# Two cross-attention layers on one core: the second layer's 256 query channels with a batch in each of two banks, projections ahead of the first layer's transposes, sums ahead of their copies

## The chip, the core and the metric

The kernel runs on one core of a Trainium2 chip, alone. The core has five engines with an instruction queue each: TensorE (PE; its weight loads are listed as PEld), VectorE (DVE), ScalarE (ACT), GpSimd (POOL) and SyncE (SP), which here only issues DMAs. The metric is the device time of one execution in microseconds (us); lower is better. Times of a kernel are given as the median of several executions.

## The reference

64 batches of 256 positions with 320 channels go through two cross-attention layers, one after the other, each with 20 heads of 16 channels and a context of 77 tokens with 512 channels.

```python
# layer 0
q = heads(x @ Wq.T); k = heads(ctx @ Wk.T); v = heads(ctx @ Wv.T)
x = merge(softmax(q k^T / 4) v) @ Wo.T + bo + x
# (its four "image" tokens are an empty slice here)

# layer 1: 73 text tokens, 4 image tokens
q = heads(x @ W_q); k_t, v_t = text @ W_k, text @ W_v; k_ip, v_ip = image @ W_k_ip, image @ W_v_ip
probs_t  = softmax(q k_t^T / 4)
text_out = probs_t v_t
sem      = l2norm(probs_t @ text) @ l2norm(image)^T
probs_ip = softmax(q k_ip^T / 4 + 0.5 * sem) * spatial_mask
out = (text_out + probs_ip v_ip) @ W_out + b_out + x
```

## The kernel before, in words

**Layout.** Channels lie on partitions. Batches are taken in pairs `p` (32 pairs). Of the 320 channels, 256 are two full tiles of 128 (`main`), and the last 64 of both batches of a pair share one tile (`last`: batch 0 in rows 0 to 63, batch 1 in rows 64 to 127). Weights have four tiles of input channels: two of 128, and two for the last 64, padded with zeros to 128 rows (rows 0 to 63 filled in one, rows 64 to 127 in the other), so that either batch can be picked out of `last` with a full K=128 matmul.

**Steps.** The main loop (L1065) runs over steps `g`. A period of ten steps (`NU`) handles one pair; `k = g % 10`, `p = g // 10`. In each step layer 0 handles one unit of pair `p` (8 heads of 128 positions; units 0 to 4 of batch 0, then of batch 1), and layer 1 handles the unit that layer 0 had 13 steps (`LAG`) before. So layer 1's units of pair `p-1` begin in `k = 3` of period `p`. A step issues, in this order: what earlier steps left (`drains`: copies of first-layer queries, or the addition after a projection); the matmuls into one four-bank tile `sc` (`semantics` of layer 1's previous unit, L755 and L761, then `scores` of both layers, L641); `shifted` on DVE (maximum and difference, L659 and L661, for each layer); layer 1's `transposed` (L705, L706, copied out by ACT at L712, L713); layer 0's exponential (L669; after layer 0's transposes in `k = 5`); `weighted` (L772, L775, DVE); the `first` fillers; layer 0's `transposed` (L705, copied out at L731, L732 or L720, L723); the copy of the sums out of `sc` (L1114, ACT, which waits until DVE's L775 is done with the tile); layer 1's exponentials (L672, L673); `normalize` (L687 and L688 on DVE, L692 on POOL); the `second` fillers; `attend` after a unit that completes a group; the `third` fillers; and after the last unit of a batch `image_norm`, which loads ACT's square-root table and then the exponential table again (L874, L876).

**Fillers.** All work that is done once per pair is spread over the steps by `fillers` (L956), a table written by hand: for each `k`, which function stands in which place (0 first, 1 second, 2 third) and for which pair.

**Order.** Engines run their instructions in the order in which the program issues them (`keep_order` at the end binds PE, ACT, DVE and POOL to it). An engine that waits holds up everything behind it in its own queue.

**PSUM.** The score tile `sc` has four banks and one buffer: the next step's `semantics` may write it only once DVE and ACT have read it. Transposes use the pool `ptr` with two banks, everything else (keys, values, queries, projections, gram matrices, `pv` of `attend`) the pool `pms` with two banks, taken in turn. So the user after next of a bank waits for whatever empties it.

**Queries.** `first_queries` (L577) makes layer 0's 256 main channels by `halves` (L520): one bank per batch, sixteen PE records at L528 over the two full tiles of input channels, and then, kept back until the start of the next step, eight records at L537, where each batch's half of `last` is a K=64 matmul in its own rows of the array. `queries(l, p, m)` (L547) makes one tile `m` of output channels at a time in one bank for both batches (L555, L557, with the zero-padded K=128 weights for `last`); `m = 2` are the last 64 channels (L563, L570). Layer 1 uses `queries` for all three tiles, layer 0 for the last one. (A matmul of these fp32 operands leaves two records.)

**Others named below.** `gram` (L484) makes a product of the context with itself that layer 1's `semantics` needs: matmuls at L493, two ACT copies, three POOL operations, one DMA at L502 and eight at L506; `place_gram` (L509) puts it into `gv` and `gr` on POOL. `project` (L590) is the output projection by `halves`, with its addition on DVE (L601) at the start of the next step; `project_last` (L609) is that of the last 64 channels, added at L620. `keys` (L326), `keys_by_head` (L360, POOL), `place_values` (L415, POOL) and `attend` (L778) are what they say. `keep_busy` (L734) issues transposes of the identity whose results nobody reads; it is used only after the last pair has entered.

Of the kernel before, what the change touches and what calls it, by code (L numbers as in the profile page):

```python
# [8 lines left out]
F32 = mybir.dt.float32  # L9
# [9 lines left out]
S = 256  # L19
T = 77  # L20
NIP = 4
TT = T - NIP
P = 128
# [14 lines left out]
HT = H - 4  # L38
NU = 2 * len(UNITS)
LAG = NU + 3  # L40
SCALE = D**-0.5
SEM = 0.5
EPS = 1e-12
# [20 lines left out]
def tile_two_cross_attentions(ctx: ExitStack, tc: tile.TileContext, a: dict, out: bass.AP):  # L64
# [35 lines left out]
    nc = tc.nc  # L100
# [443 lines left out]

    held = {}

    def queries(l, p, m):  # L547

        main, last = xts[p]
        ps = pms.tile([P, 512], F32, tag="ms", name=f"q_ps{l}_{p}_{m}")  # L550
        if m < 2:
            q = qs[l, p, m] = big.tile([P, S2], F32, tag=f"q{l}{m}", name=f"q{l}_{p}_{m}", bufs=1)
            c = slice(m * P, (m + 1) * P)
            for i in range(2):
                nc.tensor.matmul(ps, wq[l][:, i, c], main[:, i, :], start=(i == 0), stop=False)  # L555
            for b in range(2):
                nc.tensor.matmul(ps[:, b * S : (b + 1) * S], wq[l][:, 2 + b, c], last, start=False, stop=(b == 1))  # L557
            nc.scalar.copy(q, ps)
            return
        to = [ps[s * HALF : (s + 1) * HALF, :S].rearrange("p (b t) -> p b t", b=2) for s in range(2)]  # L560
        for i in range(2):
            for s in range(2):
                nc.tensor.matmul(  # L563
                    to[s], wq[l][:, i, C - HALF :],
                    main[:, i, :].rearrange("p (b s t) -> p b s t", b=2, s=2)[:, :, s, :],
                    start=(i == 0), stop=False,
                )
        for b in range(2):
            for s in range(2):
                nc.tensor.matmul(  # L570
                    to[s][:, b, :], wq[l][:, 2 + b, C - HALF :], last[:, s * P : (s + 1) * P],
                    start=False, stop=(b == 1),
                )
        q = qs[l, p, 2] = big.tile([P, 2, P], F32, tag=f"q{l}2", name=f"q{l}_{p}_2", bufs=1)
        nc.scalar.copy(q.rearrange("p b t -> p (b t)"), ps[:, :S])

    def first_queries(p):  # L577

        rest = halves(f"q_ps0_{p}", wq[0], xts[p])

        def end():
            ps = rest()
            q = big.tile([P, 2, S2], F32, tag="q0", name=f"q0_{p}")
            for m in range(2):
                qs[0, p, m] = q[:, m, :]
            return [lambda b=b: nc.scalar.copy(q[:, :, b * S : (b + 1) * S], ps[b]) for b in range(2)]  # L586

        held["q"] = end

    def project(l, p):  # L590

# [37 lines left out]
    def eight(t, u):  # L629

        return t[:, PLACES[u] : PLACES[u] + 8].rearrange("p (r e) ... -> p r e ...", e=2)
# [102 lines left out]
    def keep_busy(n):  # L734


        if n:
            ps = ptr.tile([P, 4, P], F32, tag="tr", name=f"busy{len(busy)}")
            busy.append(n)
            for i in range(n):  # L740
                nc.tensor.transpose(ps[:, i % 4, :], ident, ident)
# [24 lines left out]
    def by_block(ps):  # L766
        return ps[:, :, SEM0 : SEM0 + 2 * GV].rearrange("p r (e t) -> p r e t", t=GV)
# [93 lines left out]
    def image_least(p, b):  # L861


        total = stats[p, b][1][:, :, NIP + D]
        t = least[p, b] = small.tile([P, 2 * H], F32, tag="least", name=f"least{p}_{b}", bufs=1)
        nc.gpsimd.tensor_mul(t, total, total)
# [89 lines left out]
    def fillers(k, p):  # L956


        f = ([], [], [], [])

        def add(half, q, fn, *args):
            if 0 <= q < NP:
                f[half].append((fn, args))

        if k == 0:
            if p == 0:
                for l in range(2):
                    add(0, p, value_rows, 0, l)
                add(1, p, values, 0, p, 0)
            add(0, p - 1, gram, p - 1, 0)  # L970
            add(0, p - 3, project_last, 1, p - 3)
            add(2, p - 2, text_transposed, p - 2, 0)
            if p:
                add(2, p, place_values, 0, p, 0)
            add(2, p - 1, values, 1, p - 1, 0)
        elif k == 1:
            if p == 0:
                for l in range(2):
                    add(l, p, value_rows, 1, l)
                add(1, p, place_values, 0, p, 0)  # L980
            add(0, p, queries, 0, p, 2)
            add(1, p - 1, project, 0, p - 1)
            add(1, p - 1, place_gram, 0)
            add(1, p, keys_by_head, 0, p, 1)
            add(1, p - 1, keys_by_head, 1, p - 1, 0)
        elif k == 2:
            if p == 0:
                for i in range(2):
                    add(0, p, keys, 1, p, i)
            add(0, p - 1, project_last, 0, p - 1)  # L990
            add(1, p + 1, load_x, p + 1)
            add(1, p - 1, queries, 1, p - 1, 0)
            add(1, p - 1, place_values, 1, p - 1, 0)
            add(1, p, values, 0, p, 1)
        elif k == 3:
            add(0, p + 1, load_context, p + 1)
            add(0, p - 1, queries, 1, p - 1, 2)
            if p == 0:
                add(1, p, image_keys, 0)
            add(1, p - 1, queries, 1, p - 1, 1)  # L1000
            add(1, p, place_values, 0, p, 1)
            add(1, p - 1, keys_by_head, 1, p - 1, 1)
        elif k == 4:
            if p == 0:
                add(0, p, image_keys, 1)
            else:
                add(0, p, keys, 1, p, 0)
            add(1, p - 1, values, 1, p - 1, 1)
            add(1, p + 1, first_queries, p + 1)
        elif k == 5:  # L1010
            if p == 0:
                add(0, p, image_keys, 2)
            add(0, p + 1, keys, 0, p + 1, 0)
            add(2, p - 2, text_transposed, p - 2, 1)
        elif k == 6:
            while len(made_rows) * P < min(NB, 2 * (p + 2)) * T:
                rows_todo.extend((len(made_rows), l) for l in range(2))
                made_rows.append(rows_todo[-1])
            for n in range(len(rows_todo) // 2):
                add(0, p, value_rows, *rows_todo.pop(0))  # L1020
            if p == 0:
                add(0, p, image_norms)
            else:
                add(1, p, keys, 1, p, 1)
            add(1, p - 1, gram, p - 1, 1)
            add(1, p, place_image_keys, p)
        elif k == 7:
            add(0, p + 1, keys, 0, p + 1, 1)
            add(1, p + 1, last_keys, p + 1)
            add(1, p - 2, lambda: made.update(wT=image_transposed(p - 2)))  # L1030
            add(1, p - 1, place_values, 1, p - 1, 1)
            add(1, p - 1, image_values, p - 1, 0)
            if p == 0:
                add(1, p, image_rows)
        elif k == 8:
            while rows_todo:
                add(0, p, value_rows, *rows_todo.pop(0))
            add(1, p - 1, place_gram, 1)
            add(1, p + 1, keys_by_head, 0, p + 1, 0)
            add(1, p - 1, image_values, p - 1, 1)  # L1040
            add(1, p - 2, image_attend_last, p - 2)
            add(3, p - 2, lambda: held.update(i=lambda: image_attend(p - 2)))
        else:
            add(0, p - 2, project, 1, p - 2)
            add(1, p + 1, values, 0, p + 1, 0)
            for b in range(2):
                add(1, p - 1, place_image_values, p - 1, b)
        return f
# [7 lines left out]
        keys(0, 0, i)  # L1056
    last_keys(0)
    keys_by_head(0, 0, 0)
    first_queries(0)
    for fn in held.pop("q")():  # L1060
        fn()

    last0 = last1 = before1 = None
    later, early = {}, {}
    for g in range(NP * NU + LAG + 12):  # L1065
# [23 lines left out]
            drains += held.pop("i")()  # L1089
        for fn in drains:  # L1090
            fn()
        for l in range(2):
            if now[l]:
                shifted(ps, l, *now[l])
# [7 lines left out]
            prod = weighted(ps, *before1[:4])  # L1102
        for fn, args in first:
            fn(*args)
        if last0:
            transposed(0, *last0)
        idle = g - NP * NU
        if idle > 2:
            keep_busy(14 if now[1] else {13: 12, 14: 16, 15: 14, 16: 16, 17: 16}.get(idle, 0))
        if now[0] and k == 5:  # L1110
            exponential(0, g, *now[0])
        ends = before1 and before1[2] == len(UNITS) - 1
        if before1:
            nc.scalar.copy(eight(stats[before1[:2]][1], before1[2]), by_block(ps)[:, :, :, TT:])  # L1114
            if ends:
                image_least(*before1[:2])
        if now[1]:
            exponential(1, g, *now[1])
        for fn, args in later.pop(g, ()):
# [76 lines left out]
```

## Time and profile before

| | us |
|---|---|
| median of 3 runs | 2626.64 (2626.13 to 2627.05) |
| the profiled execution's own time | 2627.7 |
| its span in the profile | 2626.0 |
| mean granted TensorE clock | 0.996 of full speed |
| a period of ten steps in the middle (1206.56 to 1284.43) | 77.87 |

The costliest groups of the profile that the change bears on (line, engine, what, busy us in all, mean ns of one):

| line | what | records | busy us | mean ns |
|---|---|---|---|---|
| L555 | second-layer queries, full tiles, both batches (PE) | 256 | 120.6 | 593 |
| L557 | second-layer queries, padded last 64 (PE) | 256 | 68.8 | 391 |
| L528 | first-layer queries by `halves` (PE) | 512 | 116.9 | 380 |
| L537 | first-layer queries, last 64, K=64 (PE) | 256 | 36.3 | 402 |
| L493 | gram (PE) | 512 | 45.2 | 231 |
| L1114 | copy of the sums (ACT) | 320 | 96.6 | 302 |
| L874, L876 | table loads (ACT) | 128 | 164.2 | 1283 |
| L620 | addition of the last 64 channels (DVE) | 64 | 30.5 | 476 |

How to read it: the busy time of PE records overlaps, since matmuls are pipelined and their ends are modelled; the time that a group takes on PE is better read as the distance from its first start to the start of what follows. A step's length is the distance between the first L755 of two steps.

### The profile page before, as it was taken

The numbers are of one execution on the slowest core, as the hardware profiler recorded it, in microseconds if no ns is written. First come the engines' busy times: TensorE is split into PE (matmuls) and PEld (weight loads), VectorE is DVE, ScalarE is ACT, GpSimd is POOL, SyncE is SP. The second block draws the span as 40 slices with busy tenths as digits, with TensorE's granted clock in tenths as the row PEclk, the third lists the DMA queues.
The fourth block names the chain that finished last, engine by engine and source line by source line (L and its number), as shares of the span: only waits on it lengthen the run. The fifth ranks groups of instructions, "written<-read, shape, count | busy, mean of one in ns | idle before, by whom it ended". The sixth has DMA issues, their size and how long they took to land.

```text
span 2626.0 us, 74027 instructions
## 1 busy us (share of the span) xinstructions
PE 2558.2 (97%) x27006; PEld 1981.0 (75%) x27006; DVE 1972.3 (75%) x3641; ACT 1539.2 (59%) x3989; POOL 1440.1 (55%) x3514
## 2 busy tenths in 40 slices
PE   7999999999999999999999999999999999999998
PEld 5677777777777777777777777777777777777676
DVE  3577777777777777777777777777777777777764
ACT  3465665665665665665665665665665665665553
POOL 2455555565555566555566555566555556555542
PEclk9999999999999999999999999999999999999999
DMA  5212211112111112211112111112211112211000
GB/s 163 72 29 58 58 42 47 42 51 57 51 50 47 43 51 56 58 43 47 42 52 57 51 50 47 42 52 57 56 46 47 42 52 56 55 41 36 26 22 23
DMA packets 154657, 132.26 MB, mean 50 GB/s; under 512 B 48248, under 2 KB 132984, under 8 KB 154296
## 3 DMA queue, kind: packets, MB, share of 16 engines
q1 hardware_dynamic: 153432, 126.38, 17.9%
q8 instruction: 216, 3.54, 0.6%
q14 instruction: 145, 1.19, 0.2%
q10 hardware_dynamic: 864, 1.15, 0.1%
HBM read 89.53 MB, written 33.91 MB: 47 GB/s over the span
## 4 chain that ended last, share of the span: by engine, by line
PE 85%; DVE 7%; ACT 3%; DMA 2%; issue 1%; POOL 1%; SPq 1%; DVEq 0%; POOLq 0%; ACTq 0%
PE sc L755 12%; PE tr L705 11%; PE o_ps L528 8%; PE sc L641 7%; PE v_ps L379 6%; PE sc L761 4%; PE q_ps L528 4%; PE q_ps L555 4%; PE k_ps L334 4%; PE o_ps L616 3%; PE o_ps L537 3%; PE pv L788 2%; DVE w L661 2%; PE q_ps L563 2%; PE q_ps L557 2%; DVE mx L659 2%
## 5 line engine op out<-in xcount | busy, mean ns | idle before, releaser
L659 DVE TENSOR_REDUCE mx<-sc 128x8 f32<-128x584 f32 (+1 forms) x640 | 497.8, 778 | 461.1 <-PE sc L641 461.1
L692 POOL TENSOR_TENSOR parts<-w,sm 128x512 f32<-128x512 f32 (+1 forms) x640 | 439.7, 708 | 299.8 <-ACT parts L673 180.7
L661 DVE TENSOR_TENSOR w<-sc,mx 128x616 f32<-128x616 f32 x640 | 512.0, 800 | 66.7 <-DVE mx L659 0.5
L712 ACT COPY pt<-tr 128x512 f32<-128x512 f32 x320 | 186.8, 584 | 446.6 <-PE tr L705 435.0
L705 PE MATMUL tr<-ident,parts 128*128 128x128 f32 x2560 | 410.4, 283 | 11.1 <-POOL parts L692 5.3
L755 PEld LDWEIGHTS sc<-gv,pt 64*128 64x128 f32 x5120 | 317.9, 188 | 108.8 <-ACT sums L1114 60.3
L755 PE MATMUL sc<-gv,pt 64*128 64x94 f32 x5120 | 357.6, 279 | 27.9 <-ACT sums L1114 27.7
L705 PEld LDWEIGHTS tr<-ident,parts 128*128 128x128 f32 x2560 | 283.0, 141 | 122.2 <-issue 87.0
L676 POOL COPY att<-w 128x32 f32<-128x32 f32 x320 | 66.8, 209 | 471.9 <-DVE w L661 471.4
L669 ACT ACTIVATE w<-w 128x616 f32<-128x616 f32 x320 | 232.0, 725 | 96.8 <-DVE w L661 96.2
L687 DVE TENSOR_REDUCE sm<-w 128x8 f32<-128x616 f32 x320 | 248.6, 777 | 14.0 <-ACT w L669 14.0
L641 PE MATMUL sc<-kbd,q 32*128 32x154 f32 x5120 | 248.5, 306 | 1.0 <-ACT q L586 0.8
L528 PE MATMUL o_ps<-aT,wo 128*128 128x256 f32 x1024 | 233.4, 381 | 0.0
L1125 DVE TENSOR_REDUCE nrm<-prod 128x8 f32<-128x584 f32 x320 | 227.6, 711 | 0.4
L772 DVE TENSOR_TENSOR prod<-sc,parts 128x512 f32<-128x512 f32 x320 | 218.0, 681 | 4.0 <-PE sc L761 4.0
L528 PEld LDWEIGHTS o_ps<-aT,wo 128*128 128x128 f32 x1024 | 190.7, 191 | 24.0 <-DVE aT L934 0.4
L672 ACT ACTIVATE parts<-w 128x512 f32<-128x512 f32 x320 | 206.8, 646 | 0.0
L641 PEld LDWEIGHTS sc<-kbd,q 32*128 32x128 f32 x5120 | 187.3, 187 | 6.0 <-issue 5.0
L731 ACT COPY pt<-tr 128x512 f32<-128x512 f32 x256 | 150.6, 588 | 67.4 <-PE tr L705 66.7
L379 PE MATMUL v_ps<-wv,cf 128*128 128x320 f32 (+1 forms) x624 | 182.1, 438 | 0.0
L706 PE MATMUL rtr<-ident,parts 128*104 128x128 f32 (+1 forms) x640 | 175.0, 273 | 0.0
L1114 ACT COPY sums<-sc 128x168 f32<-128x168 f32 x320 | 96.6, 302 | 120.2 <-DVE prod L775 119.0
(151 smaller groups left out, 4838.5 us busy)
## 6 DMA issues: line engine op xcount, KB each, us to landing
vip<-vip_rows SPq DMA_DIRECT2D x1280, 5.0 KB
out_dram<-x SPq DMA_DIRECT2D x64, 256.0 KB
x<-in_x_dram SPq DMA_DIRECT2D x31, 512.0 KB
v_rows<-vs SPq DMA_DIRECT2D x38, 320.0 KB
vm<-v_rows SPq DMA_DIRECT2D x152, 80.0 KB
ct<-in_ctx_dram SPq DMA_DIRECT2D x32, 308.0 KB
cf<-in_ctx_dram SPq DMA_DIRECT2D x38, 256.0 KB
g_rest<-gram_rest SPq DMA_DIRECT2D x512, 0.5 KB
```

The source lines that it names most:

```text
L379: nc.tensor.matmul(ps[:n, :C], cfs[i][:, k, :n], wv[l][:, k, :], start=(k == 0), stop=(k == KE - 1))
L528: nc.tensor.matmul(ps[b][:, m, :], w[:, k, m * P : (m + 1) * P], main[:, k, b * S : (b + 1) * S], start=(k == 0 and m == 0), stop=False,)
L641: nc.tensor.matmul(ps[:, r, 2 * T * l : 2 * T * (l + 1)], q[rows, b, :] if part == 2 else q[rows, t0 : t0 + P], kbd[rows, part].rearrange( ...
L659: nc.vector.tensor_reduce(mx, sc[:, :, :, :nt], AX.X, ALU.max)
L661: nc.vector.tensor_tensor(w, sc, mx.unsqueeze(3).broadcast_to([P, 4, 2, T]), ALU.subtract)
L669: nc.scalar.activation(w, w, AF.Exp, scale=SCALE)
L687: nc.vector.tensor_reduce(sm, w, AX.X, ALU.add)
L692: nc.gpsimd.tensor_tensor(two[:, 8 * t0 : 8 * t1].rearrange("p (h t) -> p h t", h=8), w[:, :, t0:t1], sm.unsqueeze(2).broadcast_to([P, 8, ...
L705: nc.tensor.transpose(ps[:, i, :], flat[:, i * P : (i + 1) * P], ident)
L755: nc.tensor.matmul(ps[:, i % 2 * 2 + j, at : at + GV], pt[half_rows, i, :], gv[b][half_rows, part, i, :], start=start and i < 2, stop=False,)
L772: nc.vector.tensor_tensor(prod[:, :, :, :M], sm[:, :, :, :M], w[:, :4].rearrange("p (e a) j t -> p (a j) e t", e=2), ALU.mult)
L1125: nc.vector.tensor_reduce(eight(stats[q, b][2], u), prod, AX.X, ALU.add)
```

## The change

Five edits. Second-layer queries of the main 256 channels use `halves`, with one bank per batch, in one piece at the end of `k = 2` instead of a tile each in `k = 2` and `k = 3`; the function is now `queries(l, p)`, and that of the last 64 channels `last_queries(l, p)`. In `fillers`, work is moved: `gram` of batch 0 from `k = 0` to `k = 2`, `place_gram(0)` from `k = 1` to `k = 3`, the first layer's last queries from `k = 1` to `k = 3`, `project(0)` in `k = 1` and the first-layer queries in `k = 4` from behind the first layer's transposes to ahead of them, the second batch's `keys_by_head` from `k = 3` to `k = 2`, and the second layer's first tile of keys from `k = 4` to `k = 3`. In the steps `LONG` (1, 4, 8 and 9) the copy of the sums is issued ahead of the first layer's transposes and their copies. In the tail one filler (the transposes of the last pair's image weights) is issued earlier, with eight more idle transposes behind it.

```diff
+LONG = (1, 4, 8, 9)
...
-    def queries(l, p, m):
+    def last_queries(l, p):
         main, last = xts[p]
-        ps = pms.tile([P, 512], F32, tag="ms", name=f"q_ps{l}_{p}_{m}")
-        if m < 2:
-            q = qs[l, p, m] = big.tile([P, S2], F32, tag=f"q{l}{m}", name=f"q{l}_{p}_{m}", bufs=1)
-            c = slice(m * P, (m + 1) * P)
-            for i in range(2):
-                nc.tensor.matmul(ps, wq[l][:, i, c], main[:, i, :], start=(i == 0), stop=False)
-            for b in range(2):
-                nc.tensor.matmul(ps[:, b * S : (b + 1) * S], wq[l][:, 2 + b, c], last, start=False, stop=(b == 1))
-            nc.scalar.copy(q, ps)
-            return
+        ps = pms.tile([P, 512], F32, tag="ms", name=f"q_ps{l}_{p}_2")
...
-    def first_queries(p):
-        rest = halves(f"q_ps0_{p}", wq[0], xts[p])
+    def queries(l, p):
+        rest = halves(f"q_ps{l}_{p}", wq[l], xts[p])
         def end():
             ps = rest()
-            q = big.tile([P, 2, S2], F32, tag="q0", name=f"q0_{p}")
+            q = big.tile([P, 2, S2], F32, tag=f"q{l}", name=f"q{l}_{p}", bufs=2 - l)
             for m in range(2):
-                qs[0, p, m] = q[:, m, :]
+                qs[l, p, m] = q[:, m, :]
             return [lambda b=b: nc.scalar.copy(q[:, :, b * S : (b + 1) * S], ps[b]) for b in range(2)]
-        held["q"] = end
+        if l:
+            for fn in end():
+                fn()
+        else:
+            held["q"] = end
...
         if k == 0:
-            add(0, p - 1, gram, p - 1, 0)
         elif k == 1:
-            add(0, p, queries, 0, p, 2)
-            add(1, p - 1, project, 0, p - 1)
-            add(1, p - 1, place_gram, 0)
+            add(0, p - 1, project, 0, p - 1)
         elif k == 2:
-            add(1, p - 1, queries, 1, p - 1, 0)
+            add(1, p - 1, keys_by_head, 1, p - 1, 1)
+            add(1, p - 1, gram, p - 1, 0)
             add(1, p - 1, place_values, 1, p - 1, 0)
             add(1, p, values, 0, p, 1)
+            add(2, p - 1, queries, 1, p - 1)
         elif k == 3:
-            add(0, p - 1, queries, 1, p - 1, 2)
+            add(0, p - 1, last_queries, 1, p - 1)
-            add(1, p - 1, queries, 1, p - 1, 1)
+            if p:
+                add(1, p, keys, 1, p, 0)
+            add(1, p, last_queries, 0, p)
+            add(1, p - 1, place_gram, 0)
             add(1, p, place_values, 0, p, 1)
-            add(1, p - 1, keys_by_head, 1, p - 1, 1)
         elif k == 4:
-            else:
-                add(0, p, keys, 1, p, 0)
+            add(0, p + 1, queries, 0, p + 1)
             add(1, p - 1, values, 1, p - 1, 1)
-            add(1, p + 1, first_queries, p + 1)
...
+    def sums_out(ps):
+        nc.scalar.copy(eight(stats[before1[:2]][1], before1[2]), by_block(ps)[:, :, :, TT:])
+        if ends:
+            image_least(*before1[:2])
...
         for fn, args in first:
             fn(*args)
+        if before1 and k in LONG:
+            sums_out(ps)
         if last0:
             transposed(0, *last0)
         idle = g - NP * NU
         if idle > 2:
             keep_busy(14 if now[1] else {13: 12, 14: 16, 15: 14, 16: 16, 17: 16}.get(idle, 0))
+        if idle == 17:
+            fn, args = second.pop(0)
+            fn(*args)
+            keep_busy(8)
         if now[0] and k == 5:
             exponential(0, g, *now[0])
-        if before1:
-            nc.scalar.copy(eight(stats[before1[:2]][1], before1[2]), by_block(ps)[:, :, :, TT:])
-            if ends:
-                image_least(*before1[:2])
+        if before1 and k not in LONG:
+            sums_out(ps)
```

## The prediction

> **What bounds the kernel.** The page first, its busy row and its chain of waits; then TensorE's waits and the timelines of PE, DVE and ACT over one period, 1206 to 1285 us.
>
> ```profile
> PE 2558.2 (97%) x27006; PEld 1981.0 (75%) x27006; DVE 1972.3 (75%) x3641; ACT 1539.2 (59%) x3989; POOL 1440.1 (55%) x3514
> ...
> PE 85%; DVE 7%; ACT 3%; DMA 2%; issue 1%; POOL 1%; SPq 1%; DVEq 0%; POOLq 0%; ACTq 0%
> ...
> PE sc L755 <- ACT sums L1114: 27.7, 64, 2.4
> ```
>
> TensorE is the bound: no other engine is over 75% and its largest wait is 27.7 us, two per pair of batches. So a step lasts as long as PE's work in it, plus any hole. A step starts at its first L755; in this period k=4 starts at 1206.56, k=5 1215.25, k=6 1221.67, k=7 1228.62, k=8 1235.58, k=9 1243.08, k=0 1250.90, k=1 1258.97, k=2 1268.37, k=3 1276.98, the next k=4 1284.43: 77.87 us. What matters is the clock inside a step, not shares. The lines to work from (start, length, what):
>
> ```profile
> 1249.80 1.14 PE L537 MATMUL o_ps<-aT,wo 64*128 64x256 f32 x8
> 1250.90 1.13 PE L755 MATMUL sc<-gv,pt 64*128 64x94 f32 x16
> ...
> 1272.92 0.27 PE L706 MATMUL rtr<-ident,parts 128*104 128x128 f32 x1
> 1273.03 1.88 PE L555 MATMUL q_ps<-x,wq 128*128 128x512 f32 x4
> 1274.92 1.13 PE L557 MATMUL q_ps<-x,wq 128*128 128x256 f32 x4
> 1275.98 0.64 PE L788 MATMUL pv<-pt,v 128*32 128x256 f32 x8
> ...
> 1281.76 1.88 PE L555 MATMUL q_ps<-x,wq 128*128 128x512 f32 x4
> 1283.48 1.03 PE L557 MATMUL q_ps<-x,wq 128*128 128x256 f32 x4
> 1284.43 1.13 PE L755 MATMUL sc<-gv,pt 64*128 64x94 f32 x16
> ```
> ```profile
> 1270.42 0.80 DVE L659 TENSOR_REDUCE mx<-sc 128x8 f32<-128x616 f32 x1 [0.20 <-PE sc L641]
> ...
> 1274.39 0.48 DVE L620 SCALAR_TENSOR_TENSOR x<-o_ps,bo,x 128x256 f32<-128x256 f32 x1
> ```
> ```profile
> 1213.54 0.26 ACT L673 ACTIVATE parts<-w 128x72 f32<-128x72 f32 x1
> 1213.82 1.28 ACT L874 ACT_TABLE_LOAD   x1
> ...
> 1216.77 1.05 ACT L586 COPY q<-q_ps 128x512 f32<-128x512 f32 x2
> 1217.86 0.59 ACT L712 COPY pt<-tr 128x512 f32<-128x512 f32 x1
> ...
> 1221.32 0.30 ACT L1114 COPY sums<-sc 128x168 f32<-128x168 f32 x1 [0.49 <-DVE prod L775]
> ```
>
> The reader is to see three things. L557 at 1274.92 starts 0.05 after L620 ends (1274.87), because it reads what L620 wrote: DVE's place in k=2 is a real edge. ACT does the table loads of image_norm without a pause, and between L673 and the next transposed copy (L712) has no slack at all. And the sums of k=5 already wait for DVE.
>
> **The bank layout.** One old half m costs 1.72 (L555, start to L557) + 0.95 (to the next step) = 2.67; in a bare stream 1.72 + 0.86, so 5.2 for two. The new form is the one that the first layer uses: sixteen L528 records 3.55 (1210.73 to 1214.28), eight L537 0.97: 4.52. So **-0.7 per pair**, because the zero-padded K=128 matmuls become pairs of K=64 on different rows. ACT copies 2x0.59 either way.
>
> **The moves, step by step** (new length against old):
> - k=9 and k=8: sums ahead of the copies. k=8: L947 at 1242.08 is followed by the next L755 after 0.59 elsewhere, here after 1.00, since sums came behind vs, pt and pr: -0.41. k=9: L537 to L755 1.10 instead of 0.97, and the head behind it 0.11 longer: -0.24. In k=1 and k=4 no such wait exists today; there the move only covers the later transposes.
> - k=0: the gram leaves (L493 1253.52 to 1254.15): -0.63. Its two ACT copies (0.37) and three POOL operations (0.6) leave with it.
> - k=1: last_queries(0) leaves (1.45), project goes ahead of the transposes; the step becomes k=9's shape, 7.82-0.13=7.69 against 9.40: -1.71. That includes a small hole before tr at 1263.28.
> - k=3: loses 2.67, gains keys (1.00), and its head follows K=64 matmuls (0.95 instead of 1.07): new sum 1.91+0.69+1.45+0.61+1.00+1.45=7.11 against 7.45: -0.34. The scores need q at 1.5 into the step; two copies after the last L537 are done at 1.3. Cover 0.2; if gone, a wait of that size.
> - SP and POOL: gram's nine issues (SP 0.5 + 6.45) go from k=0 to k=2, past the load of x; place_gram (0.96+0.32) goes to k=3. They are issued some 10 us into k=2 and have until about 8 us into k=3; SP's next customers, vm for place_values, then have some 2 us. Behind place_gram on POOL stands only normalize of k=4, about 3 us later. Cost nothing; if late by more than that, the excess delays a transpose.
>
> **k=2, where a wait is born.** The two buffers of pms go round in order: o_ps 0, o_ps 1, o_ps 2, then g_ps, then pv. So pv takes the bank that project_last's L620 drains, and L620 stands behind mx, w, mx, w, prod on DVE. Today 2.6 us of queries stand between transposes and pv and hide it. New: PE is through the transposes at 4.66 after the step's start (1273.03), g_ps 0.63, so ready at 5.29. DVE: L601's four (1.6) now queue behind L901, as k=1 is shorter; mx starts at 2.28 instead of 2.05; L620 ends 4.45 later (1270.42 to 1274.87), pv starts at 6.78. **A hole of 1.5 us.** Queued behind pv: all of the queries and the next scores. Then pv 1.00, 3.55, 0.97: 12.30 against 8.61, +3.69, of which only 2.2 is work. Bounds of the hole: 0 if pv's DVE wait were for an older instruction, 1.0 with L601 at its old place, 1.8 if L601 is later still. I take 1.5.
>
> **k=4 and k=5, where a gain is lost.** k=4 loses keys, -1.00. But tr0 now comes after the 3.55 of queries, at 6.18; its copy can start at 6.85. From there ACT has no gap: copies and exponentials 1.45, two table loads with their two small activations 2.95, first q copy 0.58 = 11.83. k_ps of k=5 takes q_ps 0's bank, so it can start only at 11.9, while PE would be ready at 10.2: **a hole of 1.7 us**. Then ACT: second q copy, pt, pr, kT, pt, pr, w, sums, next semantics at 15.24; PE: k_ps 1.05, tr0 0.6, pv 1.0, atr 0.72: 15.3. Today the two steps take 15.11. So **+0.2 instead of -1.0**. Bounds: -1.0 (nothing held) to +0.8.
>
> [...] The row shows 1.28, and the load starts 0.02 after L673 ends: no drain. [...] by the row +0.2. I take the row.
>
> **The sum.** Per pair: -0.41-0.24-0.63-1.71+3.69-0.34+0.2 = **+0.56**. Of the 31 pairs' periods with the second layer's queries, the first has neither DVE's nor ACT's load (-1.5 there); 30 x 0.56 = +16.8. The tail: eight transposes more keep the clock from falling at 2613.1 (3.4 us at half speed, L528 5.41 instead of 3.62): -2. Net +13. Against the profiled execution (span 2626.0, its own time 2627.7) 2641; the median of the runs shown is 1.1 lower, so **2639.5 us**.
>
> [...] A hole can cost more than itself. In the last full period:
>
> ```profile
> 2473.30 2.02 PE L755 MATMUL sc<-gv,pt 64*128 64x94 f32 x16 [2.26 <-ACT sums L1114]
> ```
>
> The granted clock was 0.50 from 2473.16 to 2483.40, and the step took 10.16 instead of 6.42: +3.74. [...] the trace shows that 2.26 was enough, while 1.59 (before the filler at 2549.53) was not. [...] by the row they are too, but with 0.6 us to spare.
>
> **Rivals.**
> 1. The holes are covered: pv or k_ps finds its bank free. Without the hole of k=5 each pair is -0.64: 2604; without both -2.1: about 2561. For it: PE's 97% shows how rarely it waits today. Against: both waits follow from the order of instructions. It decides when more than 0.56 per pair of the 3.2 vanishes. **Faster**, chance 0.20.
> 2. The clock falls in the new holes. If one pair in three is hit, 10 x 3.74: 2677; in all 30, 2750. For it the row above; against it 1.59 without a drop. It decides from holes of about 2 us. Chance 0.12.
> 3. A wash: holes a third smaller, 2622 to 2632. Chance 0.14.
> 4. The forecast, 2632 to 2655: chance 0.54.
>
> A measurement of this kernel tells 0.2% (5 us) from no change. Faster 0.21, same 0.13, slower 0.66. The range 2604 to 2662 takes in rival 1's nearer end and leaves out its far end and most of rival 2.
>
> **What would show it.** L788 of k=2 waiting about 1.5 us, put down to DVE L620's line; L334 of k=5 waiting 1.7 for ACT's q copy; the wait for sums halved to k=5's 32; new query records 3.55 + 0.97 per pair; k=1 7.7, k=2 12.3, k=4 and k=5 together 15.3; period 78.4. It is wrong if PE's idle time falls, or if half-clock stretches stand in most periods.

## The result, and the profile after

The changed kernel takes **2669.82 us** (median of 5 runs, 2666.58 to 2677.31) where the kernel before takes 2626.64 (median of 5 beside it, 2626.02 to 2628.14): ratio **1.0168**, 95% interval 1.015 to 1.0186. The profiled execution took 2673.41 us with a span of 2671.6, so 45.6 us more than the span before. Its mean granted TensorE clock is 0.990, against 0.996.

The page of the changed kernel, its busy row and its chain of waits:

```profile
PE 2538.1 (95%) x27270; PEld 2032.3 (76%) x27270; DVE 1979.1 (74%) x3641; ACT 1540.8 (58%) x3989; POOL 1448.0 (54%) x3514
...
PE 70%; DVE 12%; ACT 9%; DMA 3%; issue 2%; POOL 2%; SPq 2%; DVEq 0%; ACTq 0%; POOLq 0%
```

TensorE is busy 20 us less than before, and the span is 46 us longer. In the chain, PE's share falls from 85% to 70%, and DVE and ACT gain 11 of these 15 points. TensorE's largest waits (us in total, times, longest):

```profile
PE k_ps L335 <- ACT q L578: 43.6, 29, 2.5
PE pv L784 <- DVE x L616: 39.2, 30, 1.6
PE sc L751 <- ACT sums L1059: 8.5, 6, 2.4
```

The wait for the sums went from 27.7 us to 8.5, as was meant, and from 64 times to 6 (the 32 of `k = 5`, which were expected to stay, are gone too). Two waits of 40 us each stand where there were none: once per period, in `k = 2` and in `k = 5`. The first, in PE's timeline (start, length, what, and in brackets the idle time before it with its releaser):

```profile
1215.20 0.70 PE L494 MATMUL g_ps<-ct 128*73 128x77 f32 x8
1217.20 0.64 PE L784 MATMUL pv<-pt,v 128*32 128x256 f32 x8 [1.30 <-DVE x L616]
...
1218.20 3.72 PE L529 MATMUL q_ps<-x,wq 128*128 128x256 f32 x16
1221.85 1.14 PE L538 MATMUL q_ps<-x,wq 64*128 64x256 f32 x8
1222.82 1.03 PE L751 MATMUL sc<-gv,pt 64*128 64x94 f32 x16
```

The second, on PE, in the kernel before (where nothing is waited for) and in the changed one, and on ACT:

```profile
1217.77 1.22 PE L334 MATMUL k_ps<-ct,wk 128*128 128x154 f32 x8
```
```profile
1240.12 0.27 PE L702 MATMUL rtr<-ident,parts 128*128 128x128 f32 x1
1241.78 1.32 PE L335 MATMUL k_ps<-ct,wk 128*128 128x154 f32 x8 [1.38 <-ACT q L578]
```
```profile
1238.21 1.28 ACT L870 ACT_TABLE_LOAD   x1
1239.50 0.24 ACT L870 ACTIVATE nrm<-nrm 128x40 f32<-128x40 f32 x1
1239.75 1.28 ACT L872 ACT_TABLE_LOAD   x1
1241.05 0.20 ACT L872 ACTIVATE one<-nrm 128x1 f32<-128x1 f32 x1
1241.16 1.06 ACT L578 COPY q<-q_ps 128x512 f32<-128x512 f32 x2
```

`k_ps` starts 0.6 us after L578 does: it takes the bank that the first of the two copies empties, and ACT comes to that copy straight from its table loads. In this period TensorE waits nowhere else: 2.68 us of 78.72. In a period of before the waits in the timeline come to 0.67 of 77.87. So **TensorE's own part of a period shrank from 77.20 to 76.04, and the waits grew by 2.01**.

Step by step, in us (the usual value of the 28 periods from the fourth to the thirty-first):

| k | before | after | difference | predicted |
|---|---|---|---|---|
| 0 | 8.08 | 7.51 | -0.57 | -0.63 |
| 1 | 9.40 | 7.69 | -1.71 | -1.71 |
| 2 | 8.61 | 12.26 | +3.65 | +3.69 |
| 3 | 7.45 | 7.21 | -0.24 | -0.34 |
| 4 and 5 | 15.10 | 15.36 | +0.26 | +0.2 |
| 8 | 7.51 | 7.09 | -0.42 | -0.41 |
| 9 | 7.81 | 7.69 | -0.12 | -0.24 |
| period | 77.87 | 78.72 | +0.85 | +0.56 |

Of the 45.6 us, 28 times this difference (0.844 unrounded) is 23.6. The first three periods are 8.0 longer, the tail 0.3, and 0.5 lie ahead of the first step. The remaining 13.2 are steps of the 28 periods that last longer than usual: seven instances of `k = 5` of 8.4 to 11.7 us, not 7.67, take 14.5 us more, and the other unusual steps 1.3 less than before.

In six of the seven the granted clock was halved: it was 0.50 for 3.41 us in five of them and for 6.83 in the sixth. In four the hole was longer, 2.14 to 2.47 us, and three of these are among the six. There ACT waited 0.77 to 1.10 us between its two table loads for VectorE's L866, which had waited 1.25 to 1.58 us for GpSimd's L862. GpSimd came to L862 late, since it had waited for the first layer's value rows (`vm`, `v_rest`):

```profile
514.83 0.72 POOL L454 TENSOR_TENSOR v<-vm,half 128x320 f32<-128x320 f32 x1 [4.53 <-DMA vm<-v_rows]
```

SyncE had issued these rows from 505.39 on, right behind the nine transfers of the Gram product (498.49 to 505.28) that the change has put there. The four waits at L454 are 4.53 to 4.86 us long.

Two neighbouring stretches in one of the six (length, then busy time of PE, PEld, DVE, ACT and POOL with their counts, granted clock, DMA share, GB/s), and its lines on PE:

```profile
1317.27:1320.68 3.41, 2.03 (x34) 1.53 (x33) 2.34 (x4) 3.37 (x6) 1.71 (x4) 1.00 0.01 2
1320.68:1324.09 3.41, 3.41 (x17) 2.88 (x20) 1.94 (x5) 1.63 (x5) 1.23 (x3) 0.50 0.00 0
```
```profile
1318.83 0.27 PE L702 MATMUL rtr<-ident,parts 128*128 128x128 f32 x1
1320.48 2.26 PE L335 MATMUL k_ps<-ct,wk 128*128 128x154 f32 x8 [1.38 <-ACT q L578]
```

The hole lies within the first stretch, in which PE is busy 2.03 of 3.41 us; in the next the clock is 0.50, and the same eight `k_ps` records take 2.26 us, not 1.32. This hole is no longer than the usual one.

### The profile page after: what moved, and what is told of

It is laid out like the page before. It is cut to its first block, busy times and chain, and to the rows that moved or that the text cites. A ratio compares the mean times of both kernels' runs of the same rounds, so it can differ in the third digit from the quotient of the medians.

```text
span 2671.6 us, 74517 instructions
## 1 busy us (share of the span) xinstructions
PE 2538.1 (95%) x27270; PEld 2032.3 (76%) x27270; DVE 1979.1 (74%) x3641; ACT 1540.8 (58%) x3989; POOL 1448.0 (54%) x3514
## 4 chain that ended last, share of the span: by engine, by line
PE 70%; DVE 12%; ACT 9%; DMA 3%; issue 2%; POOL 2%; SPq 2%; DVEq 0%; ACTq 0%; POOLq 0%
PE sc L751 9%; PE tr L701 9%; PE q_ps L529 8%; PE v_ps L380 6%; PE sc L637 5%; PE k_ps L335 5%; PE o_ps L529 4%; PE sc L757 3%; DVE w L657 3%; PE pv L784 3%; PE pv L789 2%; PE q_ps L555 2%; DVE mx L655 2%; ACT L872 2%; ACT L870 2%
## 5 line engine op out<-in xcount | busy, mean ns | idle before, releaser
L688 POOL TENSOR_TENSOR parts<-w,sm 128x512 f32<-128x512 f32 (+1 forms) x640 | 440.5, 710 | 347.1 <-DVE sm L684 194.6
L701 PE MATMUL tr<-ident,parts 128*128 128x128 f32 x2560 | 412.0, 284 | 12.9 <-POOL parts L688 7.1
L701 PEld LDWEIGHTS tr<-ident,parts 128*128 128x128 f32 x2560 | 288.5, 142 | 126.0 <-issue 70.0
L708 ACT COPY pt<-tr 128x512 f32<-128x512 f32 x320 | 187.4, 586 | 335.4 <-PE tr L701 329.5
L751 PE MATMUL sc<-gv,pt 64*128 64x94 f32 x5120 | 351.7, 277 | 8.6 <-ACT sums L1059 8.5
L529 PE MATMUL q_ps<-x,wq 128*128 128x256 f32 x1024 | 234.9, 382 | 0.1
L529 PEld LDWEIGHTS q_ps<-x,wq 128*128 128x128 f32 x1024 | 189.6, 190 | 36.2 <-ACT gram_rest L499 12.3
L335 PE MATMUL k_ps<-ct,wk 128*128 128x146 f32 (+1 forms) x1024 | 161.8, 302 | 50.9 <-ACT q L578 43.6
```

The lines of the kernel that those rows point to most:

```text
L335: nc.tensor.matmul(pv, wk[l][:, k, i * P : (i + 1) * P], cts[p][:, k, :, :nt], start=(k == 0), stop=(k == KE - 1))
L529: nc.tensor.matmul(ps[b][:, m, :], w[:, k, m * P : (m + 1) * P], main[:, k, b * S : (b + 1) * S], start=(k == 0 and m == 0), stop=False,)
L688: nc.gpsimd.tensor_tensor(two[:, 8 * t0 : 8 * t1].rearrange("p (h t) -> p h t", h=8), w[:, :, t0:t1], sm.unsqueeze(2).broadcast_to([P, 8, ...
L701: nc.tensor.transpose(ps[:, i, :], flat[:, i * P : (i + 1) * P], ident)
L751: nc.tensor.matmul(ps[:, i % 2 * 2 + j, at : at + GV], pt[half_rows, i, :], gv[b][half_rows, part, i, :], start=start and i < 2, stop=False,)
```

## The experiments

Each number is the median of 4 to 14 executions, timed beside the kernel before. "Ratio" is against that kernel, with its 95% interval; the changed kernel itself is 1.0168. The groups e1 to e5, e6 to e9, e10 to e12 and e14 were timed on different chips, where the kernel before took 2625.7 to 2627.9 us: a difference between groups of 2 us means nothing. "The late value" below is the value of L862 in the four periods named above.

| kernel | median us | ratio |
|---|---|---|
| e1, query projection late again | 2653.6 | 1.0098 (1.0082 to 1.0115) |
| e2, bank drained first in `k = 2` | 2673.7 | 1.0170 (1.0152 to 1.0187) |
| e3, e1 and e2 | 2656.4 | 1.0111 (1.0096 to 1.0126) |
| e5, hole of `k = 5` filled | 2661.6 | 1.0127 (1.0112 to 1.0143) |
| e6, Gram product back | 2640.0 | 1.0056 (1.0043 to 1.0069) |
| e7, query copies on VectorE | 2635.6 | 1.0035 (1.0021 to 1.0048) |
| **e8, e6 and e7** | **2604.8** | **0.9919 (0.9905 to 0.9932)** |
| e9, before with the sums ahead | 2617.6 | 0.9969 (0.9957 to 0.9980) |
| e10, e8 with a filler in `k = 2` | 2615.3 | 0.9954 (0.9942 to 0.9967) |
| e11, e8 without unit 1's sums | 2609.4 | 0.9935 (0.9922 to 0.9947) |
| e12, before with two units' sums ahead | 2616.1 | 0.9959 (0.9945 to 0.9973) |
| e14, e8 with the old query banks | 2631.1 | 1.0016 (1.0008 to 1.0024) |

### The holes, first attempt: e1, e2, e3

```diff
-LONG = (1, 4, 8, 9)
+LONG = (1, 8, 9)
...
-            add(0, p + 1, queries, 0, p + 1)
             add(1, p - 1, values, 1, p - 1, 1)
+            add(1, p + 1, queries, 0, p + 1)
```

> The changed kernel with one part undone: in unit 4 the first layer's query projection for the next pair goes back behind the first layer's transposes (among the fillers that follow them), and so does the copy of the sums of that unit. Theory 1 (the hole): the projection ahead of the transposes makes their ScalarE copies some 3.5 us later, the query copies then come late, and unit 5's key projection waits 1.4 us for the bank. Undone, that wait goes, units 4 and 5 take about 14.3 us together and not 15.36, and the halvings of the clock in unit 5 (about 14 us of the run) go with it: 2671.6 - 31 - 14 = about 2626 us. Rival (the longer periods come from the other moves, and the clock's drops from the chip): units 4 and 5 stay within 0.2 us of 15.36 and the time at 2660 us or above.

Measured: 2653.6 us. The wait in `k = 5` and every halving in a steady period went (the granted clock of its runs is 0.994 to 0.995), but `k = 4` and `k = 5` take 8.59 + 6.42 = 15.01 together, 0.35 less and not 1.06: `k = 5` lost 1.25 and `k = 4` gained 0.90. That is 10 us for 28 periods; the halvings are the larger part of what else the profile lost. So the hole is real, but putting the projection back isn't the way to get its price: that order has its own waits, 0.71 us in `k = 4` for ACT's copy of the transposes and 0.33 us for the sums.

```diff
+        if k == 2:
+            for fn, args in first:
+                fn(*args)
         if before1:
             prod = weighted(ps, *before1[:4])
-        for fn, args in first:
-            fn(*args)
+        if k != 2:
+            for fn, args in first:
+                fn(*args)
```

> The changed kernel with one VectorE instruction moved: in unit 2 the addition that drains the bank of the last projection (project_last) stands ahead of the two products of the second layer's weights, not behind them. TensorE's order is the same. Theory 2: in unit 2 the value product (pv) waits 1.3 to 1.6 us for the bank that this addition empties, and the two products stand in its way; the wait shrinks by about their 0.9 us in each of 30 periods: -27 us, about 2644 us, with the halvings of the clock in unit 5 still there. Rival (the wait is a slack that something later would have cost anyway): the wait shrinks, and the products' later end moves the time of unit 2 or 3 by as much: 2667 to 2673 us.

Measured: 2673.7 us, and `k = 2` 12.35, so nothing gained. PE's timeline of this kernel says why:

```profile
1213.98 0.70 PE L494 MATMUL g_ps<-ct 128*73 128x77 f32 x8
1215.24 0.64 PE L784 MATMUL pv<-pt,v 128*32 128x256 f32 x8 [0.57 <-DVE x L616]
...
1217.07 3.72 PE L529 MATMUL q_ps<-x,wq 128*128 128x256 f32 x16 [0.75 <-ACT gram_rest L499]
```

The addition is earlier and `pv` waits 0.57, not 1.30. Then the queries, next in the row, take the bank of the Gram product, and wait 0.75 us for ACT to copy that: 1.32 in all. My theory had named one drain; there are two banks in turn with two late drains, by two engines. (The rival had the time right, with another place.)

> Both edits together: the query projection of unit 4 and its sums' copy behind the first layer's transposes, and in unit 2 the bank's addition ahead of the two products. If the two holes are separate costs, their gains add: 2626 - 27 = about 2599 us, below both kernels. If they share a cause, no more than the larger of the two: about 2625 us.

Measured: 2656.4 us, 2.8 more than e1; e2 adds nothing to it either.

### The clock by itself: e5

```diff
+        if l and k == 5:
+            for i in range(9):
+                nc.tensor.transpose(pr[:, 1 + i % 3, :], ident, ident)
```

> The changed kernel with nine more transposes of the identity in unit 5 of every period, written into unused columns of the bank of the second layer's last transpose, so that TensorE works through about 1.35 us of the 1.4 to 1.7 us in which it waits for the query copy. They add no result. If the halvings of the clock in unit 5 are set off by this hole and cost 14 us beside it, the step lengths stay (period 78.7 us), the halvings of unit 5 go, and the time is about 2657 us with a spread between runs of about 2 us. If the halvings have another cause, they stay and the time is 2667 to 2677 us. If the copy of the transposes waits for the extra ones, it is slower.

```profile
1238.39 1.15 PE L705 MATMUL rtr<-ident 128*128 128x128 f32 x9
1239.93 1.32 PE L335 MATMUL k_ps<-ct,wk 128*128 128x154 f32 x8 [0.40 <-ACT q L578]
```

Measured: 2661.6 us, 2660.24 to 2661.92. In this timeline the nine transposes fill all but 0.40 us of the hole. The usual period is 78.72 as before, and no halving is left between 162 and 2510 us. The mean granted clock of its runs is 0.994 to 0.995, that of the changed kernel's 0.988 to 0.992. So the halvings come from the hole, and cost about **8 us of the median** (11 by the two ratios). Four instances of `k = 5` are still 0.70 to 0.97 us long here, at full clock: those with the late value. They come to 3.5 us; in the profiled execution of the changed kernel some 11 of the 14.5 us are then left for the halvings. In three of the six the late value had lengthened the hole. The halvings are also what scatters the changed kernel's runs: 10.7 us between the ends without the filler, 1.7 with it.

### The holes by their causes: e6, e7, e8

```diff
 # k == 0
+            add(0, p - 1, gram, p - 1, 0)
             add(0, p - 3, project_last, 1, p - 3)
 # k == 1
             add(0, p - 1, project, 0, p - 1)
+            add(1, p - 1, place_gram, 0)
 # k == 2
-            add(1, p - 1, gram, p - 1, 0)
 # k == 3
-            add(1, p - 1, place_gram, 0)
```

> The changed kernel with the Gram product put back where it was before (unit 0, its placing in unit 1); queries, keys and sums stay as changed. Moving one VectorE drain ahead did not shorten unit 2: the wait went over to the query product, which then waited 0.75 us for ScalarE's copy of the Gram product. Theory 2b: there are two buffers in turn, and in unit 2 four products take them in a row behind two late drains; with the Gram product out of this row, the value product takes a bank that was free long before. Then unit 2 loses the Gram product's 0.7 us and the 1.3 us of wait (12.26 to about 10.3), unit 0 gains 0.6 (7.51 to about 8.1): -1.4 us per period, about 2669.8 - 42 = 2628 us. Rival: the query product then waits for the last projection's bank as long as the value product did: unit 2 at 11.6, no gain, about 2670 us.

Measured: 2640.0 us: -0.64 per period. `k = 0` is 7.97 (+0.46) and `k = 2` 11.17 (-1.09), not 10.3:

```profile
1199.98 0.27 PE L702 MATMUL rtr<-ident,parts 128*104 128x128 f32 x1
1200.82 0.64 PE L784 MATMUL pv<-pt,v 128*32 128x256 f32 x8 [0.56 <-ACT pt L727]
```

The bank is free now, and `pv` meets what was hidden behind it: its own operand, the copy of the transposes just made. That is the next wait in line, and half of the expected gain went into it and into 0.16 us between `pv` and the queries. This kernel also shows where the late value came from. GpSimd's wait for the value rows is short again, and no `k = 5` of the 28 periods is long:

```profile
504.52 0.72 POOL L454 TENSOR_TENSOR v<-vm,half 128x320 f32<-128x320 f32 x1 [0.96 <-DMA vm<-v_rows]
```

In the same four periods this wait is 0.74 to 2.63 us, and L866 waits 0.11. The late value is gone from every kernel here that has the Gram product back (e6, e8, e10, e11, e14), and stands in the same four periods of those that have it as changed (e1, e2, e3, e5, e7).

```diff
-            return [lambda b=b: nc.scalar.copy(q[:, :, b * S : (b + 1) * S], ps[b]) for b in range(2)]
+            copy = nc.scalar.copy if l else nc.vector.tensor_copy
+            return [lambda b=b: copy(q[:, :, b * S : (b + 1) * S], ps[b]) for b in range(2)]
```

> The changed kernel with the first layer's two query copies of a period on VectorE, not ScalarE; nothing else moves. Theory 1b (from the trace: putting the projection back gave units 4 and 5 together only 0.35 us): the hole of unit 5 comes from the copy's place in ScalarE's queue, behind a chain of copies, exponentials and two table loads. On VectorE, which idles 1.03 us there while it waits for the scores, the copy ends before TensorE asks for the bank: unit 5 falls from 7.67 to about 6.3 us, its clock halvings go (8 us, as the filled hole showed), and the time is about 2669.8 - 1.4 x 30 - 8 = 2620 us. Rival: VectorE's later maxima take back what the copies give (about 0.3 us later each), or the chain on ScalarE holds the next transposes anyway: unit 5 above 7.2 us, 2650 us or more.

Measured: 2635.6 us. DVE's timeline, then PE's:

```profile
1222.21 0.39 DVE L818 RECIPROCAL rec<-sums 128x40 f32<-128x40 f32 x1
1222.53 1.21 DVE L579 COPY q<-q_ps 128x512 f32<-128x512 f32 x2
1223.66 0.78 DVE L656 TENSOR_REDUCE mx<-sc 128x8 f32<-128x616 f32 x1
```
```profile
1224.10 1.22 PE L335 MATMUL k_ps<-ct,wk 128*128 128x154 f32 x8
1225.74 0.63 PE L702 MATMUL tr<-ident,parts 128*128 128x128 f32 x4 [0.42 <-ACT pt L709]
```

The copies lie where DVE had waited for the scores, `k_ps` waits for nothing, and `k = 5` is 6.63: -1.04, with 0.42 us of a new wait for a bank of the transposes. Nor is the clock halved in a steady `k = 5` any more (0.994 to 0.995 in its runs). Of the gap to the expected 2620, 11 us are that smaller step (0.36 x 30). Four instances of `k = 5` that take 8.2 to 8.5 us at full clock are another 7, somewhat more than the rest. In the one that was followed, VectorE waited 1.41 us for GpSimd's L863 ahead of these copies: the late value again, at a place where it costs more.

> The Gram product back in unit 0 and the query copies on VectorE, both in the changed kernel. In the trace of a steady period of the changed kernel TensorE waits only at these two places, 2.68 us of 78.72; before, it waited 0.67 of 77.87. So the change saved 1.16 us of TensorE time per period and paid 2.0 us of waits. With both waits gone the period is about 76.0 us, 1.8 below the kernel before: 2627 - 1.8 x 30 + some 8 us that the first two periods cost more = about 2580 us. If the waits only move elsewhere: 2610 us or more.

Measured: **2604.8 us, 0.8% below the kernel before**. The gains add: -0.64 and -1.04 make -1.67 of the period, now 77.04. No steady `k = 5` is long. TensorE's waits in this kernel:

```profile
PE pv L785 <- ACT pt L728: 18.9, 32, 1.1
PE tr L702 <- ACT pt L709: 14.8, 33, 0.7
PE sc L752 <- ACT sums L1060: 8.2, 6, 2.4
```

The two waits of 40 us are gone; two of 15 and 19, both for copies of transposes, stand behind them, and they are why it isn't the expected 2580.

### Parts of the change by themselves: e9, e12, e14

The kernel before with the sums' copy moved as in the change (`sums_out` and `LONG`, the tail apart), first for all four units, then for 8 and 9:

```diff
+        if before1 and k in LONG:
+            sums_out(ps)
         if last0:
             transposed(0, *last0)
```

> The kernel before with one part of the change alone: the copy of the sums ahead of the first layer's transposes' copies in units 1, 4, 8 and 9. By the prediction's reading the scores of units 2, 5, 9 and 0 wait less for it; units 8 and 9 measured 0.42 and 0.12 us shorter in the changed kernel, and 0.32 to 0.35 us of waits for the sums stand in two of the units of before. Expected -0.5 to -0.9 us per period, 2600 to 2612 us. Rival: ScalarE's copies of the transposes come later by the sums' 0.3 us and hold the value product: no gain, 2622 to 2632 us.

> The kernel before with the sums' copy ahead in units 8 and 9 alone. The four units together gave 8 us of time: units 0, 8 and 9 became 0.10, 0.42 and 0.12 us shorter, unit 1 became 0.34 longer. If unit 1's loss is its own copy's, it goes and the gain is 0.64 us per period: about 2607 us. If it is pushed over from unit 0, unit 1 stays at 9.74 us and the time at about 2618 us.

Measured: 2617.6 and 2616.1 us, with the same steps to 0.01 us: `k = 0` -0.10, `k = 8` -0.42, `k = 9` -0.12, and `k = 1` **+0.35**. So this part is worth 8 us, not 20; units 1 and 4 have no part in it; and `k = 1` isn't longer by its own copy, since e12 left it behind. It hands back half of what the three steps ahead of it gained (0.64). The trace of e12 shows the edge: the first layer's transposes of `k = 1` wait 0.42 us for L713, ACT's copy of the second layer's transposes, and ACT comes to that copy from L894, ahead of which it waited 2.84 us for GpSimd's L891 (2.50 in the kernel before). A step that starts earlier gains nothing against that. In the changed kernel the projection stands ahead of these transposes, and `k = 1` is 7.69 as predicted.

```diff
-            add(2, p - 1, queries, 1, p - 1)
+            add(2, p - 1, whole_queries, p - 1)
```

(`whole_queries` is the old form, a bank for each 128 channels, for both tiles.)

> The version with both holes removed, with the second layer's queries in their old form again: a bank for each 128 channels with both batches in it, both in unit 2 at the place of the new form. The prediction put the new form at 0.7 us less per period. If that holds with no wait in the way, unit 2 becomes 11.17 + 0.7 = about 11.9 us and the time 2604.8 + 0.7 x 30 = about 2626 us. Rival: the form makes no difference where it stands (the shorter records are only another count), and the time stays at 2602 to 2610 us.

```profile
1200.40 1.98 PE L576 MATMUL q_ps<-x,wq 128*128 128x512 f32 x4
1202.22 1.03 PE L578 MATMUL q_ps<-x,wq 128*128 128x256 f32 x4
1203.08 1.88 PE L576 MATMUL q_ps<-x,wq 128*128 128x512 f32 x4
1204.80 1.03 PE L578 MATMUL q_ps<-x,wq 128*128 128x256 f32 x4
1205.75 1.13 PE L764 MATMUL sc<-gv,pt 64*128 64x94 f32 x16
```

Measured: 2631.1 us. The old form takes 1205.75 - 1200.40 = 5.35 us, where the new one takes 4.62 in the timeline shown above (1222.82 - 1218.20): +0.73 in `k = 2`, and `k = 3` is 0.10 longer. **The bank layout is worth 26 us by itself** (25.5 by the ratios), the largest gain among the parts tried, and the two holes hid it.

### Attempts at more: e10, e11

```diff
 # k == 2
+            add(1, p, last_queries, 0, p)
 # k == 3
-            add(1, p, last_queries, 0, p)
```

> The version with both holes removed (Gram product in unit 0, query copies on VectorE), and the first layer's last 64 query channels moved from unit 3 to unit 2, between the transposes and the value product. There the value product still waits 0.56 us for ScalarE's copy of the transposes; 1.6 us of queries would cover it. Theory: the wait goes, unit 2 takes about 12.2 us (11.17 + 1.6 - 0.56), unit 3 about 5.6, and the time is 2604.8 - 0.56 x 30 = about 2588 us. Rival: it puts one more product into the row of two buffers, so the value product takes the bank of the last projection again, or the query product waits for the copy of the moved queries: no gain, or up to 1 us per period lost (2605 to 2635 us).

Measured: 2615.3 us. `k = 2` +1.09, `k = 3` only -0.72. One product more in the row of banks, and `pv` waits 0.36 us for the last projection's addition again. And `k = 3` stops at 6.49, since the scores then wait 0.66 us for the sums, whose copy comes after VectorE's four maxima and differences and two products (1200.49 to 1204.54 in the timeline of this kernel, the copy at 1204.58). So moving 1.6 us of TensorE's work out of this step shortened it by 0.72 only; the chain on VectorE held it.

```diff
-LONG = (1, 4, 8, 9)
+LONG = (4, 8, 9)
```

> The version with both holes removed, with the sums' copy of unit 1 back behind the copies of the transposes; units 4, 8 and 9 stay ahead. With the sums moved alone, unit 1 of the kernel before became 0.34 us longer. If that is the sums' copy of unit 1 itself holding the transposes' copies, this gains up to 0.34 us per period (2595 us). If unit 1 of the changed kernel (7.69 us, only structure left) has room for it, nothing changes or the scores of unit 2 wait up to 0.35 us for it (2605 to 2615 us).

Measured: 2609.4 us; `k = 1` +0.03 and `k = 2` +0.10. In this version unit 1's copy is better ahead.

## Why the prediction had the holes right and the time wrong

The sign was right, and so were the places of both waits and the two instructions that release them. The time was not: 2669.8 us lies above the range that was given, 2604 to 2662, and the spans differ by 45.6 us where +13 was forecast. By its steps:

- **The two holes: right in place and cause.** 1.5 us was taken in `k = 2`, and 1.30 shows in the period above; 1.7 in `k = 5`, and 1.38 shows. The work in these steps was larger by nearly as much (the queries of `k = 2` take 4.62 us, not 4.52), so that the steps came out within 0.06 us is in part luck. That both holes are costs in themselves is shown by e6, e7 and e8: without them the kernel beats the one before. The table loads took what the row of before had shown, 1.28 us each, with nothing beside it: in ACT's lines above the activation starts 0.01 or 0.02 us after the load ends, and the two steps grew by 0.26 us.
- **The bank layout: right.** -0.7, and e14 shows 0.73 + 0.10.
- **The period: 0.29 too low.** +0.85, not +0.56. The Gram product's leaving was put at -0.63 in `k = 0`; e6, which brings it back, lengthens that step by 0.46. Another 0.10 lies in `k = 3` and 0.06 in `k = 4` and 5. The sums in `k = 8` and 9 were right: of the -0.65 forecast, -0.42 and -0.12 show there and -0.10 in the head of `k = 0` (e9 has the same three). In the kernel before, `k = 1` takes 0.35 of that back (e9). Over 28 periods the error is 8 us.
- **"With 0.6 us to spare": this step failed.** The prediction held its holes, 1.5 and 1.7 us, to be too short to set off a halving. It compared a hole's length with one hole that had set off a halving (2.26 us) and one that had not (1.59). In the steady periods of the profile 1.38 us set it off three times of 24, and of the four longer holes three did, while one of 2.14 us did not. Length alone doesn't decide. e5 shows what it costs, 8 us of the median. Rival 2 had the mechanism, with a chance of 0.12, and too high a price: 3.74 us per hit came from a drop of 10.24 us, while five of the six here last 3.41 us, and a hit in a usual period costs 1.6 us (9.28 or 9.29 against 7.67).
- **"SP and POOL ... Cost nothing": this failed too, in four periods.** The prediction named the danger: the Gram product's nine transfers stand in SyncE's queue ahead of `vm`, and if late by more than some 2 us, "the excess delays a transpose". In the four periods with the late value `vm` came to GpSimd 7.1 to 7.4 us after the start of `k = 4`; in e6, without the Gram product there, 2.1 to 4.0. The excess delayed not a transpose but L862, and through L866 and the table loads the same query copy that holds `k_ps`. At full clock this costs 3.5 us in all (e5), and three of the six halvings came with these longer holes.
- **The start: wrong sign.** -1.5 was put for the first pair's period, and the first three are 8.0 us longer. In this profile about 3.8 of these are half clock (0.50): a stretch at 81.64 us that the kernel before doesn't have (2.0), and one at 149.91 that lasts 10.24 us where that of the kernel before lasts 6.83 (1.8). The third period has the usual 0.85 on top. In the first two the trace shows new waits of TensorE: in `k = 3` of the first 1.14 us for GpSimd's L688, in a step that begins 1.05 us earlier than before, and 0.47 for a query copy (L567); in `k = 2` and 3 of the second 0.54 for a copy of transposes (L727), then 0.29 and 0.47 for query copies. I had taken the steady moves without their holes. This is read from the trace; no experiment tried the start by itself, so what set off its halvings stays open.
- **The tail: -2 was not there in this profile.** It came from a halving at 2613.1 us that the eight extra transposes should have kept away; the profile after has one at 2658.7 (0.50 for 3.41 us, as before), 12.9 us from the end in both. Whether the edit can keep it away in another execution was not shown.

Together: 23.6 against 16.8 for the periods, 13.2 against 0 for the long instances of `k = 5` and the other unusual steps, 8.0 against -1.5 for the start, 0.3 against -2 for the tail, and 0.5 ahead of the first step.

Rival 1 (the holes are covered) fell in this kernel. Its number for both holes gone, 2561, fell too: e8 gave 2604.8, since behind each hole stood a smaller one that the longer wait had hidden.

## What to carry to other kernels

Buffers that are handed out in turn tie each product to one that came two places earlier: before work is moved into such a row, write out which drain each later product then waits for, and on which engine that drain queues. Moving a late drain within its queue only passed the wait on here (e2); what helped was to take a product out of the row (e6), or to give the drain to an engine that idles at that moment (e7). Moved work takes its transfers along: look at what stands behind them in the queue of the engine that issues them. And a sum of holes is not the whole of their price: look for the wait that stands next behind each of them, and count a possible clock drop by its share of periods.

## What the runs showed of the hardware

In the changed kernel's profile the six halvings of the steady periods follow holes of 1.38 us (three times), 2.20, 2.27 and 2.47 us, all shorter than the stretch of low clock behind them. The starts of these halvings lie whole multiples of 3.41 us apart (760.89 and 842.81 are 24 of them; 842.81 and 1320.68 are 140), and they last one or two such units.

Divided into stretches of 3.41 us that are counted from these starts, the 28 periods of this profile have 651 at full clock. In 22 of them PE is busy for 2.04 us or less, and all six halvings follow one of these: three of the four with 1.1 to 1.7 us, and three of the 18 with 2.02 to 2.04 us, in which a usual hole lies whole. None of the six follows a stretch with more (the one in the tail, at 2658.7, does: 3.07 us). After the other 15 of the 18 the clock stays at 1.00; and in the period of e6's timeline, which kept the hole of `k = 5` with 1.38 us, the eight `k_ps` records behind it take 1.32 us, as at full clock. So in this profile PE's busy time in a stretch tells where the six could come, but not where they did; what decides that stays open. That filling the hole ends the halvings is shown by e5: the hole is 0.40 us there, and the granted clock of its runs 0.994 to 0.995.
